# Bringing the score maxima of a two-stage attention kernel to rows through DRAM, beside the queries, with new first loads, fillings and ranks

## Chip, cores, metric

One core of a Trainium2 chip. The metric is the device time of the whole program in microseconds, the median of the runs shown. Engines are named as in the profile: PE (TensorE matmuls), PEld (its weight loads), DVE (VectorE), ACT (ScalarE), POOL (GpSimd), SP (SyncE, which here only issues DMAs).

## What is computed

16 sequences of 256 tokens, width 256, each with a context of 77 rows, all in float32. A first block applies to each sequence self-attention (16 heads of 16), cross-attention to its context and a gated MLP of width 1024, each with an RMS norm and a residual. A second block lets each normalised token attend to the normalised context (one head of 256), puts the result through a 4-wide GELU bottleneck, normalises, attends to itself and adds up.

```python
def attention(x, ctx, wq, wk, wv, wo):
    q = (x @ wq).reshape(B, S, NH, HD)
    k = (ctx @ wk).reshape(B, Skv, NH, HD)
    v = (ctx @ wv).reshape(B, Skv, NH, HD)
    scores = jnp.einsum('bqhd,bkhd->bhqk', q, k) * HD ** (-0.5)
    attn = jax.nn.softmax(scores.astype(jnp.float32), axis=-1)
    out = jnp.einsum('bhqk,bkhd->bqhd', attn, v).reshape(B, S, NH * HD)
    return out @ wo
...
h = residual + attention(h, h, sa_wq, sa_wk, sa_wv, sa_wo)
h = residual + attention(hn, context, ca_wq, ca_wk, ca_wv, ca_wo)
h = residual + mlp(hn, w_gate, w_up, w_down)
```

## The kernel before

**Stages.** Sequences (`b`, 0 to 15) go in pairs (`u`, UB = 2). The work of a sequence is cut into generators: `self_operands` (norm, transposition, q, k, v: tiles psq, psk, psv), `self_maxima`, `exponentials`, `outputs`, `projection` (wo), the same for the cross-attention (`cross_keys`, `cross_queries`, `cross_maxima`, tiles with a leading c), `mlp` (pg, pu, wd) and, per pair, `second_context` and `second`, which stores the result (L1192).

**The order** of all engines' instructions is written at build time by `Order.run` (L340). Each generator yields a `Step`: its PE time, its shape (f: full 128x128 array; r: four 32-row tiles; c: four 32-column tiles), the PSUM banks, the times of the other engines' instructions, what it needs and gives, and a lag. `Order` keeps a clock for each engine and takes the PE step that can start without being late, lowest rank first; the rank is the sequence number plus the stage's entry in `RANKS` (three numbers: always, for sequences 0 and 1, for the last three), plus `STANDS_BACK` for some changes of shape. `T_TURN` (L230) is the planned cost of a change of shape. Steps of other engines are put in between when they end within 500 ns of the best PE step's end (L360). SP's queue is in that order too: an issue that waits holds up all behind it. Where PE would wait, `keep_busy` (L326) issues matmuls on the identity (fillings, tile idle, L335).

**Softmax maxima.** Scores are computed twice. First with queries as rows (sc, L574, and csc, L600, row tiling: 32 rows for two heads), so that DVE can take each query's maximum, negated (L579, L607). The maxima of one sequence stand in a tile nmax, [128, 2, 128], query p of half i in partition p, with zeros between the 16 heads' columns. `maxima_rows` (L546) transposes both halves on PE (L551) into a bank, and two DVE instructions (L553) multiply that by the head masks and add it into qx, the masked queries, into rows which are zero there. kx holds ones in those rows, so the second score matmul (st and cst, L635; keys as rows) gives score minus maximum, and ACT's exponential (L643) writes pT, which `outputs` (L677) uses as it is. The four score banks (tile sc) are shared by all these and by parts of `second`.

**Transposed activations.** For sequences 0 and 1 `feature_major` transposes the normalised tokens on PE (L218). For all others DVE transposes 32x32 blocks (L429), SP writes them to DRAM (L434) and reads them back with the blocks in place (L439); the result is hnT. In the self-attention's hnT the two 128-feature chunks alternate element by element, in the others they stand 32 by 32. `project_T` reads hnT as the moving operand, `tokens_moving` in token order; psv reads it as weights (L748).

**First loads.** SP issues the four x tiles of sequences 0 and 1 with the first contexts between (L102 to L105). ACT's queue issues wq, wk, wv and wo (L152 to L155), POOL's sa_nw (L145), SP the rest. `weights` multiplies the norms' weights into the matrices (L1209). ACT's first own work is the square in `rmsnorm` (L377); the rstd in it is a power on POOL (L210), which also fills tiles by memset (L186 to L192).

Of the kernel before, what the change touches and what calls it, by code (L numbers as in the profile page):

```python
# [15 lines left out]
P = 128  # L16
D = 256
# [12 lines left out]
def kernel(  # L30
# [71 lines left out]
    for t in range(NT):  # L102
        if t == QT:
            cxs[0] = load_context(0, UB, "cx")
        load_tokens(0, t)  # L105

# [35 lines left out]

    ident = const.tile([P, P], F32, tag="ident", name="ident")
    make_identity(nc, ident)
    sa_nw = load_columns(sa_norm_w, "sa_nw", nc.gpsimd, True)  # L145
# [6 lines left out]
    wq = load_matrix(sa_wq, "wq", nc.scalar, True)  # L152
    wk = load_matrix(sa_wk, "wk", nc.scalar, True)
    wv = load_matrix(sa_wv, "wv", nc.scalar, True)
    wo = load_matrix(sa_wo, "wo", nc.scalar)  # L155
# [29 lines left out]
    for i in range(2):  # L185
        t = const.tile([SK, NH, 2 * HD], F32, tag=f"cvone{i}", name=f"cvone{i}")  # L186
        nc.gpsimd.memset(t, 1.0)
        cvones.append(t)
    for i in range(4):
        t = const.tile([P, QT, P], F32, tag=f"nmax{i}", name=f"nmax{i}")  # L190
        nc.gpsimd.memset(t, 0.0)
        maxes[i % 2].append(t)  # L192
# [42 lines left out]
    STANDS_BACK = {"rf": 5, "cf": 5, "fc": 10}  # L235
# [17 lines left out]
    class Order:  # L253
# [72 lines left out]
        def keep_busy(self, t):  # L326

            bank, after = self.banks["mm"][:2]
            n = int((t - self.clock["P"] - 350) / T_IDLE) if self.clock["P"] else FIRST_IDLE
            if n < 2 or None in bank + after or max(bank + after) > self.clock["P"]:  # L330
                return
            rows, cols = slice(RG if self.shape == "r" else P), slice(RG if self.shape == "c" else P)
            ps = mm_bank("idle")
            for _ in range(n):
                nc.tensor.matmul(  # L335
                    ps[cols, :P], lhsT=ident[rows, cols], rhs=ident[rows], start=True, stop=True
                )
            self.banks["mm"] = self.banks["mm"][1:] + [[t]]

        def run(self):  # L340
            while self.streams:
                best = None
                aux = []
                for st in self.streams:
                    t = self.start(st)
                    if t is None:
                        continue
                    if st.step.pe:
                        turn, wait = self.shape + st.step.shape, t - self.clock["P"]
                        late = wait > 100  # L350
                        rank = st.rank[0] + STANDS_BACK.get(turn, 0) + 0.05 * wait
                        key = (late, t + T_TURN[turn] if late else 0, rank, st.rank[1])
                        if best is None or key < best[0]:
                            best = (key, st, t)
                    else:
                        e = st.step.ops[0][0]
                        aux.append((max(t + T_NEXT, self.clock[e]), st.rank, st, t))
# [36 lines left out]
    def tokens_moving(t, c):  # L394

        return t[:, :, :, c].rearrange("p a i t -> p i a t")

# [148 lines left out]
    def maxima_rows(a, nm):  # L546

        yield Step(QT * T_TR, ops=[("V", 690), ("V", 690)], gives=[a.key("mT")])
        tp = mm_bank(f"{a.name}tm{a.b}")
        for i in range(QT):  # L550
            nc.tensor.transpose(tp[:, i * P : (i + 1) * P], nm[:, i, :], ident)  # L551
        for e in range(2):
            nc.vector.scalar_tensor_tensor(  # L553
                a.qx[:, :, e], bc_mid(tp[:, :S], NC), head_mask[:, 1 - e : 2 - e],
                a.qx[:, :, e], ALU.mult, ALU.add,
            )

    def maxima_of(nm, qt):

        return nm[:, qt].rearrange("p (j n d) -> p j n d", j=4, n=2 * NC)[:, :, :, 0]  # L560

    def self_maxima(a):
        for qt in range(QT):
            for c in range(NC):
# [4 lines left out]
                nm = maxes[0][a.b % 2]  # L569
                sc = sc_banks(f"sc{a.b}_{qt}{c}")  # L570
                for e in range(2):
                    for j in range(4):
                        rg = slice(RG * j, RG * (j + 1))
                        nc.tensor.matmul(  # L574
                            sc[:, j, (1 - e) * S : (2 - e) * S],
                            lhsT=a.qx[rg, c, e, qt * P : (qt + 1) * P],
                            rhs=a.kx[rg, c, e], start=True, stop=True,
                        )
# [9 lines left out]
    def cross_maxima(a):  # L588
        for qt in range(QT):
# [5 lines left out]
            nm = maxes[1][a.b % 2]  # L595
            sc = sc_banks(f"csc{a.b}_{qt}")
            for c in range(NC):
                for j in range(4):
# [5 lines left out]
                        lhsT=a.q[rg, c, qt * P : (qt + 1) * P],  # L604
# [84 lines left out]
    def projection(a):  # L689
# [21 lines left out]
        for i in range(QT):  # L711
# [11 lines left out]
    def self_operands(a):  # L723
# [3 lines left out]
        ps = yield from project_T(wq, lambda c: tokens_moving(hnT, c), S, f"psq{b}", in_halves(  # L727
# [64 lines left out]
    def cross_queries(a):  # L792
# [3 lines left out]
        ps = yield from project_T(cwq, lambda c: tokens_moving(hnT, c), S, f"pscq{b}", in_halves(  # L796
# [212 lines left out]
    def second(n, u, first, nb):  # L1009
# [164 lines left out]
        for kc in range(QT):  # L1174
            for t in range(NT):
# [37 lines left out]
    def context_loads():  # L1213
        for u in range(NU):
            yield Step(
                ops=[("S", 100)], acq=[("cx", u)], gives=[("cx", u)], lag=4000 if u else 6000
# [4 lines left out]
    def second_loads():  # L1221
        for u in range(NU):
            yield Step(ops=[("S", 100)], acq=[("cx2", u)], gives=[("cx2", u)], lag=4000)
            cx2s[u] = load_context(UB * u, UB, "cx2")
# [3 lines left out]
        ("x", 0): 5e3, ("x", 1): 20e3, "wq in": 8e3, "wk in": 9e3, "wv in": 10e3, "cwk": 12e3,  # L1228
# [19 lines left out]
        "mlp": (4.25, 2.75, -2.5),  # L1248
        "second_context": (5.5, 0, -50),
        "second": (3, 0, -50),  # L1250
# [71 lines left out]
```

## Time and profile before

| what | value |
|---|---|
| median of 3 runs | 995.84 us (995.49 to 997.2) |
| the profiled execution | 996.82 us, span 995.0 |
| mean granted clock of PE | 0.989 |
| busy PE / PEld / DVE / ACT / POOL | 97 / 72 / 63 / 48 / 9 % of the span |
| L551, maxima transposed on PE | 64 matmuls, 7.2 + 6.4 us busy |
| L553, maxima added into qx | 64 on DVE, 0.71 to 0.75 us each |
| L335, fillings | 198 matmuls, 32.5 us busy |
| DMA | 39.61 MB, mean 40 GB/s |

The span runs from the first to the last instruction. PE's matmuls are pipelined and their ends are modelled, so the time that one block of matmuls takes is better read as the distance from its start to the start of the next block than as its busy time. Instructions of float32 matmuls come in twos: eight make a projection of 256 x 256 for 256 tokens. Starts are in us from the span's beginning.

### The profile page before, as it was taken

To read this page: it belongs to the slowest core of one execution; us is meant where nothing else is said; L and a number is where in the kernel's file an instruction comes from. 1 tells how busy PE (TensorE), PEld (TensorE's weight loads), DVE (VectorE), ACT (ScalarE), POOL (GpSimd) and SP (SyncE) were. 2 spreads that over 40 slices of the span, in tenths; PEclk is the share of its full clock that TensorE was granted. 3 is DMA by queue.
4 is the path that set the end of the run, shared out by engine and by line. 5 is a ranking of instruction groups with operands and counts; after the bars stand their busy time and mean duration, and the time that the engine had idled before them with its cause. 6 is when DMAs were issued, how large, how long until landed. Compare 5 with 4: busy or idle time off the path is not lost.

```text
span 995.0 us, 18977 instructions
## 1 busy us (share of the span) xinstructions
PE 968.8 (97%) x8136; PEld 715.0 (72%) x8136; DVE 622.7 (63%) x1075; ACT 475.7 (48%) x770; POOL 93.7 (9%) x124
## 2 busy tenths in 40 slices
PE   7989999999999999999999999999999999999997
PEld 6766666676776667777776777777677777778876
DVE  4865576666675657766676655775578565655552
ACT  4246645334555364543755354454571526543432
POOL 2510000000010010100100000010020000100210
PEclk9899999999999999999999999999999999999997
DMA  8301001001000111002100121011210110001000
GB/s 275 82 24 39 22 11 40 2 22 32 29 23 22 42 61 43 12 33 77 43 12 22 46 83 46 1 33 35 64 54 1 49 33 23 32 12 54 12 22 22
DMA packets 45732, 39.61 MB, mean 40 GB/s; under 512 B 4336, under 2 KB 39760, under 8 KB 45648
## 3 DMA queue, kind: packets, MB, share of 16 engines
q1 hardware_dynamic: 44448, 37.34, 11.8%
q8 instruction: 64, 1.05, 0.4%
q10 hardware_dynamic: 1136, 1.05, 0.3%
q14 instruction: 20, 0.16, 0.1%
q0 software_dynamic: 64, 0.00, 0.0%
HBM read 23.14 MB, written 15.20 MB: 39 GB/s over the span
## 4 chain that ended last, share of the span: by engine, by line
PE 86%; DMA 4%; DVE 4%; ACT 4%; issue 1%; ACTq 0%; POOL 0%; SPq 0%; POOLq 0%
PE pg L828 11%; PE pu L828 11%; PE wd L858 11%; PE sc L574 6%; PE st L635 6%; PE po L677 5%; PE cst L635 3%; PE psq L499 3%; PE pscq L499 3%; PE wo L716 3%; PE cpo L677 3%; PE cwo L716 3%; PE psk L499 3%; PE psv L748 2%; PE csc L600 2%; ACT pT L643 2%
## 5 line engine op out<-in xcount | busy, mean ns | idle before, releaser
L579 DVE TENSOR_REDUCE nmax<-sc 128x8 f32<-128x2048 f32 x64 | 146.6, 2290 | 39.3 <-PE sc L574 39.2
L643 ACT ACTIVATE pT<-st 128x2048 f32<-128x2048 f32 x64 | 120.1, 1877 | 100.9 <-PE st L635 100.7
L828 PE MATMUL pg<-hnT_mlp,wg 128*128 128x256 f32 x512 | 129.8, 387 | 0.0
L828 PE MATMUL pu<-hnT_mlp,wu 128*128 128x256 f32 x512 | 128.7, 387 | 0.5 <-DVE sg L839 0.5
L858 PE MATMUL wd<-wd,gT 128*128 128x256 f32 x512 | 126.3, 388 | 0.0
L828 PEld LDWEIGHTS pu<-hnT_mlp,wu 128*128 128x128 f32 x512 | 93.4, 190 | 22.9 <-issue 10.6
L858 PEld LDWEIGHTS wd<-wd,gT 128*128 128x128 f32 x512 | 92.6, 190 | 23.8 <-issue 11.9
L828 PEld LDWEIGHTS pg<-hnT_mlp,wg 128*128 128x128 f32 x512 | 92.6, 190 | 21.0 <-issue 9.5
L643 ACT ACTIVATE cpT<-cst 77x2048 f32<-77x2048 f32 x32 | 59.9, 1872 | 59.2 <-PE cst L635 59.2
L838 ACT ACTIVATE sg<-pg 128x512 f32<-128x512 f32 x64 | 38.2, 597 | 101.5 <-PE pg L828 101.3
L839 DVE SCALAR_TENSOR_TENSOR sg<-sg,pg 128x512 f32<-128x512 f32 x64 | 43.9, 686 | 67.2 <-ACT sg L838 66.7
L677 PE MATMUL po<-pT,vone 128*32 128x256 f32 x1024 | 62.7, 382 | 0.1
L840 DVE SCALAR_TENSOR_TENSOR gT<-sg,pu 128x512 f32<-128x512 f32 x64 | 43.7, 683 | 28.5 <-PE pu L828 27.4
L607 DVE TENSOR_REDUCE nmax<-csc 128x16 f32<-128x1232 f32 x32 | 46.1, 1440 | 8.3 <-PE csc L600 8.0
L677 PEld LDWEIGHTS po<-pT,vone 128*32 128x32 f32 x1024 | 29.7, 109 | 26.0 <-issue 9.7
L210 POOL TENSOR_TENSOR rstd_n<-ve_n,neg_half 128x4 f32<-128x4 f32 (+3 forms) x28 | 23.4, 837 | 206.2 <-DVE ve_n L208 160.6
L210 POOL TENSOR_TENSOR rstd_ca<-ve_ca,neg_half 128x2 f32<-128x2 f32 x16 | 11.1, 697 | 304.7 <-DVE ve_ca L208 304.6
L335 PE MATMUL idle<-ident 128*128 128x128 f32 (+2 forms) x198 | 32.5, 327 | 2.5 <-POOL ident masks.py:199 2.5
L499 PE MATMUL pscq<-hnT_ca,cwq 128*128 128x256 f32 x128 | 31.7, 388 | 2.4 <-DMA hnT_ca<-blocks_ca 2.4
L499 PE MATMUL psk<-hnT_sa,wk 128*128 128x256 f32 x128 | 33.4, 397 | 0.0
L499 PE MATMUL psq<-hnT_sa,wq 128*128 128x256 f32 x128 | 33.4, 399 | 0.0
L335 PEld LDWEIGHTS idle<-ident 128*128 128x128 f32 (+2 forms) x198 | 30.7, 228 | 3.5 <-POOL ident masks.py:199 2.5
(614 smaller groups left out, 1570.8 us busy)
## 6 DMA issues: line engine op xcount, KB each, us to landing
h<-in_x_dram SPq DMA_DIRECT2D x7, 512.0 KB
blocks_sa<-hb_sa SPq DMA_DIRECT2D x14, 256.0 KB
hnT_sa<-blocks_sa SPq DMA_DIRECT2D x14, 256.0 KB
blocks_ca<-hb_ca SPq DMA_DIRECT2D x14, 256.0 KB
hnT_ca<-blocks_ca SPq DMA_DIRECT2D x14, 256.0 KB
blocks_mlp<-hb_mlp SPq DMA_DIRECT2D x14, 256.0 KB
hnT_mlp<-blocks_mlp SPq DMA_DIRECT2D x14, 256.0 KB
out_dram<-h SPq DMA_DIRECT2D x7, 512.0 KB
```

What stands on the lines that cost most here:

```text
L335: nc.tensor.matmul(ps[cols, :P], lhsT=ident[rows, cols], rhs=ident[rows], start=True, stop=True)
L499: nc.tensor.matmul(ps[:, m * n : (m + 1) * n], lhsT=w[:, c, m * P : (m + 1) * P], rhs=src(c), start=(c == 0), stop=(c == NC - 1),)
L574: nc.tensor.matmul(sc[:, j, (1 - e) * S : (2 - e) * S], lhsT=a.qx[rg, c, e, qt * P : (qt + 1) * P], rhs=a.kx[rg, c, e], start=True, stop=True,
L579: nc.vector.tensor_reduce(maxima_of(nm, qt)[:, :, c::NC], sc.rearrange("p j (y k) -> p j y k", y=2), AX.X, ALU.max, negate=True,)
L607: nc.vector.tensor_reduce(maxima_of(nm, qt), sc[:, :, : 2 * NC * SK].rearrange("p j (n k) -> p j n k", k=SK), AX.X, ALU.max, negate=True,)
L635: nc.tensor.matmul(st[:nk, j, e * S : (e + 1) * S], lhsT=a.kx[rg, c, e, kc * P : kc * P + nk], rhs=a.qx[rg, c, e], start=True, stop=True,)
L643: nc.scalar.activation(a.pT[k][:nk].rearrange("p j e q -> p j (e q)"), st[:nk], AF.Exp, scale=HD ** -0.5,)
L677: nc.tensor.matmul(po[RG * j : RG * (j + 1), e, :], lhsT=a.v[:nk, kc, 8 * c + 2 * j + e, :], rhs=pT[:nk, j, e, :], start=(kc == 0 and e == ...
L716: nc.tensor.matmul(ps[:, i * D : (i + 1) * D], lhsT=oT[:, c, i * P : (i + 1) * P], rhs=a.w[:, c, :], start=(c == 0), stop=(c == NC - 1),)
L828: nc.tensor.matmul(ps[:, i * S : (i + 1) * S], lhsT=w[:, c, (f + i) * P : (f + i + 1) * P], rhs=tokens_moving(hnT, c), start=(c == 0), sto ...
L839: nc.vector.scalar_tensor_tensor(sg, sg, 1.0, ps, ALU.add, ALU.mult)
L858: nc.tensor.matmul(ps[:, :D], lhsT=gT[:, f, i * P : (i + 1) * P], rhs=wd[:, f, :], start=(f == 0), stop=(f == NF - 1),)
```

## The change

The maxima of sequences 2 to 15 no longer go through PE. Their nmax is [128, 2, 32] with 16 used columns; DVE transposes it in 32x32 blocks, SP writes it to DRAM, and four SP reads put the rows straight into the zero rows of qx. Query position 2p+i now holds token 128i+p (`tokens_paired`, and steps of two, `qt::QT`, in the weight loads that must give token order back). Sequences 0 and 1 keep the transposition on PE, with their four wide nmax in one tile.

```diff
     def maxima_rows(a, nm):
-        yield Step(QT * T_TR, ops=[("V", 690), ("V", 690)], gives=[a.key("mT")])
-        tp = mm_bank(f"{a.name}tm{a.b}")
-        for i in range(QT):
-            nc.tensor.transpose(tp[:, i * P : (i + 1) * P], nm[:, i, :], ident)
...
+        if a.b < UB:
+            yield Step(QT * T_TR, ops=[("V", 690), ("V", 690)], gives=[a.key("mT")])
+            tp = mm_bank(f"{a.name}tm{a.b}")
+            for i in range(QT):
+                nc.tensor.transpose(tp[:, i:S:QT], nm[:, i, :], ident)
...
+            return
+        name = f"{a.name}nm{a.b}"
+        yield Step(ops=[("V", 140)])
+        nb = small.tile([P, RG, QT], F32, tag="nmb", name=f"{name}b")
+        nc.vector.transpose(nb.rearrange("p t i -> p i t"), nm)
+        yield Step(ops=[("S", 500)], gives=[name], lag=2000)
+        rows = dram.tile([P, RG * QT], F32, tag="rows", name=f"{name}r")
+        nc.sync.dma_start(rows, nb.rearrange("p t i -> p (t i)"))
+        yield Step(ops=[("S", 2000)], needs=[name], gives=[a.key("mT")], lag=2000)
+        by_row = rows.rearrange("(g w) x -> w g x", w=RG)
+        for n in range(2 * NC):
+            y, c = divmod(n, NC)
+            nc.sync.dma_start(
+                a.qx[RG // 4 * n :: RG, c, 1 - y].rearrange("j (g x) -> j g x", x=RG * QT),
+                by_row[n : 8 * NC : 2 * NC],
+            )
...
+    def tokens_paired(t, c):
+        return t[:, :, :, c].rearrange("p a i t -> p a t i")
...
-                            lhsT=a.qx[rg, c, e, qt * P : (qt + 1) * P],
+                            lhsT=a.qx[rg, c, e, qt::QT],
...
-                        lhsT=a.q[rg, c, qt * P : (qt + 1) * P],
+                        lhsT=a.q[rg, c, qt::QT],
...
-                    ps[:, i * D : (i + 1) * D], lhsT=oT[:, c, i * P : (i + 1) * P],
+                    ps[:, i * D : (i + 1) * D], lhsT=oT[:, c, i::QT],
...
-        ps = yield from project_T(wq, lambda c: tokens_moving(hnT, c), S, f"psq{b}", in_halves(
+        ps = yield from project_T(wq, lambda c: tokens_paired(hnT, c), S, f"psq{b}", in_halves(
...
-        ps = yield from project_T(cwq, lambda c: tokens_moving(hnT, c), S, f"pscq{b}", in_halves(
+        ps = yield from project_T(cwq, lambda c: tokens_paired(hnT, c), S, f"pscq{b}", in_halves(
```

The first loads are in another order: SP takes the two x tiles of sequence 0, then sa_nw, wk, wv, the x tiles of sequence 1, the contexts and wo; ACT's queue keeps only wq.

```diff
+    for t in range(QT):
+        load_tokens(0, t)
...
+    wq = load_matrix(sa_wq, "wq", nc.scalar, True)
+    sa_nw = load_columns(sa_norm_w, "sa_nw", nc.sync, True)
+    wk = load_matrix(sa_wk, "wk", nc.sync, True)
+    wv = load_matrix(sa_wv, "wv", nc.sync, True)
+    for t in range(QT, NT):
+        load_tokens(0, t)
+    cxs[0] = load_context(0, UB, "cx")
+    wo = load_matrix(sa_wo, "wo", nc.sync)
...
+    wide = pool.tile([P, 4, QT, P], F32, tag="lp", name="nmax", bufs=1)
+    nc.gpsimd.memset(wide, 0.0)
```

In the planner: fewer fillings in long gaps and some in shorter ones; no T_TURN in the choice among late steps; SP's steps stand aside while PE's clock is behind them; 800 for 500; the out store is a step of its own; other due times of the first loads; other ranks.

```diff
-    STANDS_BACK = {"rf": 5, "cf": 5, "fc": 10}
+    STANDS_BACK = {"rf": 5, "cf": 5, "fc": 5}
...
-            n = int((t - self.clock["P"] - 350) / T_IDLE) if self.clock["P"] else FIRST_IDLE
-            if n < 2 or None in bank + after or max(bank + after) > self.clock["P"]:
+            n = int((0.7 * (t - self.clock["P"]) - 150) / T_IDLE) if self.clock["P"] else FIRST_IDLE
+            if n < 1 or None in bank + after or max(bank + after) > self.clock["P"]:
...
-                        key = (late, t + T_TURN[turn] if late else 0, rank, st.rank[1])
+                        key = (late, t if late else 0, rank, st.rank[1])
...
+                        b = max(t + T_NEXT, self.clock[e])
+                        (ahead if e == "S" and b > self.clock["P"] else aux).append(
+                            (b, st.rank, st, t)
+                        )
+                if not best and not aux:
+                    aux = ahead
...
-                    if best is None or b + sum(o[1] for o in st.step.ops) <= best[2] + best[1].step.pe + 500:
+                    if best is None or b + sum(o[1] for o in st.step.ops) <= best[2] + best[1].step.pe + 800:
...
-        yield Step(460, "r", "sc", ops=[("V", 70 + 290 * NT)], rel=[("h", u)] * (first + nb == UB),
-                   gives=[("second", n)])
+        yield Step(460, "r", "sc", ops=[("V", 70 + 290 * NT)], gives=[("second", n)])
         nc.vector.tensor_tensor(h, h, by_rows(zT, k["last"], "out"), ALU.add)
+        yield Step(ops=[("S", 600)], rel=[("h", u)] * (first + nb == UB), lag=3000)
         nc.sync.dma_start(tokens(out, u)[:, first * QT : first * QT + NT], h)
...
-        "second_constants": (1, 50, 0),
-        "outputs": (6.5, -1, 50),
+        "second_constants": (-49, 0, 0),
+        "outputs": (6.5, -51, 50),
...
-        "projection": (-0.5, -50, -0.5),
-        "cross_outputs": (5, 0, 0.25),
+        "projection": (-0.5, -50, 1.5),
+        "cross_outputs": (5, 2, 0.25),
...
-        "cross_projection": (-50.5, 0, 50),
-        "self_maxima": (-0.25, -50, -100),
-        "cross_maxima": (-49, 0, 0),
-        "cross_queries": (-2, 1, -49.5),
-        "self_operands": (-2, 0, -0.5),
-        "cross_keys": (1.75, 0, 0),
-        "mlp": (4.25, 2.75, -2.5),
-        "second_context": (5.5, 0, -50),
-        "second": (3, 0, -50),
+        "cross_projection": (-51.5, 0, 50),
+        "self_maxima": (-0.25, -50, -101),
+        "cross_maxima": (-99, 0, 0),
+        "cross_queries": (1, -49, -49.5),
+        "self_operands": (-2, 0, 0.5),
+        "cross_keys": (0.75, 0, 2),
+        "mlp": (4, 0.75, 0.5),
+        "second_context": (5.5, 0, 0),
+        "second": (5, 0, -50),
```

More of the change, by code (lines that the diff above doesn't have):

```diff
@@ L100, in load_context @@
         return t
[L102 to L105, printed above, removed]
     def tokens_of(b):
@@ L141, in row @@
         return src.rearrange("(o d) -> o d", o=1)
+    for t in range(QT):
+        load_tokens(0, t)
     ident = const.tile([P, P], F32, tag="ident", name="ident")
     make_identity(nc, ident)
-    sa_nw = load_columns(sa_norm_w, "sa_nw", nc.gpsimd, True)
+    wq = load_matrix(sa_wq, "wq", nc.scalar, True)
[6 more added lines that the diff above has]
+    wo = load_matrix(sa_wo, "wo", nc.sync)
     vones, cvones, maxes = [], [], ([], [])
@@ L151 @@
         vones.append(t)
[L152 to L155, printed above, removed]
     load_tokens(1)
@@ L188 @@
         cvones.append(t)
+    rows_of = ([], [])
+    wide = pool.tile([P, 4, QT, P], F32, tag="lp", name="nmax", bufs=1)
+    nc.gpsimd.memset(wide, 0.0)
     for i in range(4):
-        t = const.tile([P, QT, P], F32, tag=f"nmax{i}", name=f"nmax{i}")
+        maxes[i % 2].append(wide[:, i])
+        t = const.tile([P, QT, RG], F32, tag=f"nmax{i}", name=f"nmax{i}")
         nc.gpsimd.memset(t, 0.0)
-        maxes[i % 2].append(t)
+        rows_of[i % 2].append(t)
     def bc_mid(t, n):
@@ L342, in run @@
                 best = None
-                aux = []
+                aux, ahead = [], []
                 for st in self.streams:
@@ L356, in run @@
                         e = st.step.ops[0][0]
-                        aux.append((max(t + T_NEXT, self.clock[e]), st.rank, st, t))
+                        b = max(t + T_NEXT, self.clock[e])
[4 more added lines that the diff above has]
+                    aux = ahead
                 if aux:
                     b, _, st, t = min(aux, key=lambda a: a[:2])
-                    if best is None or b + sum(o[1] for o in st.step.ops) <= best[2] + best[1].step.pe + 500:
+                    if best is None or b + sum(o[1] for o in st.step.ops) <= best[2] + best[1].step.pe + 800:
                         self.put(st, t)
@@ L546, in maxima_rows, with maxima_tile @@
     def maxima_rows(a, nm):
-        yield Step(QT * T_TR, ops=[("V", 690), ("V", 690)], gives=[a.key("mT")])
-        tp = mm_bank(f"{a.name}tm{a.b}")
-        for i in range(QT):
[L551 to L555, printed above, removed]
-            )
+        if a.b < UB:
[3 more added lines that the diff above has]
+                nc.tensor.transpose(tp[:, i:S:QT], nm[:, i, :], ident)
+            for e in range(2):
+                nc.vector.scalar_tensor_tensor(
+                    a.qx[:, :, e], bc_mid(tp[:, :S], NC), head_mask[:, 1 - e : 2 - e],
+                    a.qx[:, :, e], ALU.mult, ALU.add,
+                )
[14 more added lines that the diff above has]
+                by_row[n : 8 * NC : 2 * NC],
+            )
+    def maxima_tile(a):
+        return (maxes if a.b < UB else rows_of)[bool(a.name)][a.b % 2]
     def maxima_of(nm, qt):
-        return nm[:, qt].rearrange("p (j n d) -> p j n d", j=4, n=2 * NC)[:, :, :, 0]
+        wide = nm.shape[-1] == P
+        return nm[:, qt, : P if wide else 16].rearrange(
+            "p (j n d) -> p j n d", j=4, n=2 * NC
+        )[:, :, :, 0]
     def self_maxima(a):
@@ L568, in self_maxima @@
                 )
-                nm = maxes[0][a.b % 2]
+                nm = maxima_tile(a)
                 sc = sc_banks(f"sc{a.b}_{qt}{c}")
@@ L594, in cross_maxima @@
             )
-            nm = maxes[1][a.b % 2]
+            nm = maxima_tile(a)
             sc = sc_banks(f"csc{a.b}_{qt}")
@@ L1215, in context_loads @@
             yield Step(
-                ops=[("S", 100)], acq=[("cx", u)], gives=[("cx", u)], lag=4000 if u else 6000
+                ops=[("S", 100)], acq=[("cx", u)], gives=[("cx", u)], lag=(10000, 20000)[u] if u < 2 else 4000
             )
@@ L1222, in second_loads @@
         for u in range(NU):
-            yield Step(ops=[("S", 100)], acq=[("cx2", u)], gives=[("cx2", u)], lag=4000)
+            yield Step(ops=[("S", 100)], acq=[("cx2", u)], gives=[("cx2", u)], lag=4000 if u > 1 else 20000)
             cx2s[u] = load_context(UB * u, UB, "cx2")
@@ L1227 @@
     order.done.update({
-        ("x", 0): 5e3, ("x", 1): 20e3, "wq in": 8e3, "wk in": 9e3, "wv in": 10e3, "cwk": 12e3,
+        ("x", 0): 4e3, ("x", 1): 20e3, "wq in": 5e3, "wk in": 6e3, "wv in": 7e3, "cwk": 12e3,
         "cwv": 13e3, "cwq in": 16e3, "wg in": 24e3, "wu in": 27e3, "wd": 24e3, "late": 14e3,
```

## Prediction

> **What bounds the kernel now.** I read the page's busy times first, then the busy times by stretch, then TensorE's own timeline, then the start and the end. The profiled execution took 996.82 us with a span of 995.0, so 1.82 us lie outside the span; the median of the runs shown is 995.84. I work out differences in the span and take them off the median.
>
> ```profile
> PE 968.8 (97%) x8136; PEld 715.0 (72%) x8136; DVE 622.7 (63%) x1075; ACT 475.7 (48%) x770; POOL 93.7 (9%) x124
> ...
> DMA  8301001001000111002100121011210110001000
> ```
>
> Only PE is full. VectorE has a third of the span free and the DMA engines are nearly idle after the first two slices: a change that moves work from PE to those two pays if nobody waits for the detour.
>
> ```profile
> 0.00:25.00 25.00, 19.81 (x116) 17.09 (x116) 11.18 (x28) 11.69 (x29) 5.69 (x18) 1.00 0.90 274
> ...
> 300.00:400.00 100.00, 99.87 (x854) 71.77 (x852) 63.78 (x109) 51.43 (x83) 6.22 (x9) 1.00 0.13 42
> ...
> 950.00:995.00 45.00, 36.77 (x212) 28.63 (x210) 17.81 (x61) 10.81 (x20) 3.76 (x5) 0.84 0.07 24
> ```
>
> The columns are stretch, length, busy PE, PEld, DVE, ACT, POOL, granted clock, DMA share, GB/s. In the middle PE never stops, so only removed PE time counts there. The ends are chains: PE idles, or runs the fillings of L335, which the first column counts as busy.
>
> **Part 1: maxima of sequences 2 to 15 leave PE.** 14 sequences x 2 attentions = 28 blocks of two transposes (L551) go. What one is worth is read from starts, since PE durations overlap:
>
> ```profile
> 154.29 1.03 PE L828 MATMUL pu<-hnT_mlp,wu 128*128 128x256 f32 x4
> 155.15 0.38 PE L551 MATMUL tm<-ident,nmax 128*128 128x128 f32 x2
> 155.46 1.15 PE L574 MATMUL sc<-kx__973,qx__907 32*128 32x256 f32 x16
> ```
>
> The block holds PE from 155.15 to 155.46, 0.31 us. But four pu matmuls before a full-array successor take 0.86 (154.29 to 155.15) and before a row-tiled one 0.95 (171.40 to 172.35): 0.09 of the 0.31 is the turn to row tiling, which the block before will then pay. So 0.22 each, and 28 x 0.22 = **6.1 us** saved. Blocks that follow a row-tiled step hold 0.27 and leave their turn to their successor in the same way.
>
> On VectorE 28 x 2 x 0.745 (the STTs of L553) = 41.7 us go. 28 small transposes come: 128x128 takes 0.31 and 128x512 0.70 (L1151, L429), so a line through both gives 0.25 for 64 columns, 7 us in all. VectorE is no bound; I count nothing, between 0 and -2.
>
> New on SP: one write and four reads per block, 140 DMAs. An issue takes 0.33 (L434) to 0.73 (L923), so 46 to 102 us of a queue that issued some 120 DMAs and mostly waits. The reads wait for the write to land; behind them on SP stand loads of hnT, for which PE waits. A 256 KB write lands 2.0 us after its issue when nothing disturbs it (the chain shows 3.5), its read after 2.7 (chain: 2.9 to 3.9). Path from the last maximum to usable rows: 0.25 + 0.35 + 2.0 + 4 x 0.33 + 2.7 = 6.6 us, where the transposes and STTs needed some 2 to 3. I read for each of the 28 the end of its last maximum and the start of its first score matmul (L635): 12 have over 6.6 us already, 16 have 2.3 to 5.9. Those 16 lack 39 us together. The order gives each step a due time, and mlp, projection and output matmuls of other sequences stand ready, so I take 0 with bounds 0 and +39. Without that cover it is rival B.
>
> The out store becomes a step of its own and SP steps are put off while PE is behind them, so that SP is less often parked in front of a load. PE waits that ended with a load of hnT_ca sum to 2.4 us and psq's weight load waited 0.4. I take **-1.2**, bounds -2.8 and 0; the loss side is B's.
>
> **Part 2: queries in pairs.** So that one row of a DRAM block is 64 neighbouring positions, position 2p+i holds token 128i+p. Three readers change.
> (a) The weight loads of sc, csc and wo step by 8 bytes. psv does that today: 195 ns against 189 for pscq, and its matmuls keep their pace. In wo it is hidden; in 64 sc and 32 csc visits at most one 6 ns load is in front: **+0.6**, bounds 0 and +2.3 (four loads in front).
> (b) The moving operand of psq and pscq (128 instructions each) now jumps 256 bytes back and forth. No row shows PE reading so. Nearest: psq already steps by 8 bytes and pscq does not; from 183.20 to 185.11 psq needs 1.91 per eight, pscq 1.80 (169.60 to 171.40), both after a row-tiled step and before a full one. By start-to-start that is 10 to 14 ns per instruction for half the neighbours. I price the next halving alike: +10 on psq, +20 on pscq, 128 x 0.010 + 128 x 0.020 = **+3.8 us**. Lower end 0 (a moving read can't gain from jumps). Upper end: ACT's L387 for sequences 0 and 1 reads and writes in 16-byte steps and takes up to 0.758 where the plain one takes 0.50: 0.25 per 256 elements, 256 x 0.25 = +64. I keep near the PE row, since it is the same engine and the same line.
>
> A rule speaks against (b). The Trainium skill, "SBUF — State Buffer", section "Door 1: The DMA port swizzle", says that SBUF has lines of 16 bytes, that at least two consecutive hits on a line are needed for full rate, and that each access to another line pays. The paired read has one hit per line; psq's 8-byte step has two and should be free by the rule, where the row shows 10 ns. The page gives no price; at half rate for PE it would make the sum rival A's 1037, by the PE row 986.
>
> **Part 3: the start.** ACT's queue issues wq, wk, wv and wo, and only then its first work:
>
> ```profile
> 0.75 1.28 ACTq L116 DMA_DIRECT2D wq<-in_L_xattn_sa_wq_dram  x2
> ...
> 6.98 0.41 ACTq L120 DMA_DIRECT2D wo<-in_L_xattn_sa_wo_dram  x1
> 7.42 1.28 ACT L377 ACT_TABLE_LOAD   x1 [7.42 <-DMA wv<-in_L_xattn_sa_wv_dram]
> ...
> 8.71 0.42 ACT L377 ACTIVATE sq_sa<-h 128x256 f32<-128x256 f32 x1
> ...
> 13.26 2.05 PE L499 MATMUL psq<-hnT_sa,wq 128*128 128x256 f32 x8
> ```
>
> With wq alone on it, ACT is free at 2.03, the table is loaded by 3.3 and the square can start there: the first x tile, issued at 0.74, landed at 2.8. From square to psq takes 4.55, so psq at about 8; rstd on POOL then queues behind the memsets (to 5.0 now; one wide one and four small more, but sa_nw's 1.3 of issuing gone) and may lose half a microsecond: 8.5 instead of 13.26, 4.7 earlier. sa_nw, now on SP, is due at 5 to 5.5 and does not bind. The price is the second pair of x tiles, cx and wo behind wk and wv. What follows (scores, maxima, exponentials up to 130) is a dependent chain and should shift along; I count **-4.0**, bounds -4.7 and 0 (DMA is 90% busy to 25, so something later may arrive no earlier).
>
> **Part 4: fillings.** Their number falls from (gap-350)/220 to (0.7 gap-150)/220. Two hold up work now:
>
> ```profile
> 975.50 6.15 PE L335 MATMUL idle<-ident 128*128 128x128 f32 x32
> ...
> 978.84 0.25 DVE L1113 COPY mga<-mg 128x12 f32<-128x12 f32 x2
> 981.48 0.27 PE L1124 MATMUL tp_g2T<-ident,g 128*64 128x128 f32 x1
> ```
>
> The operands are there at 979.1, PE comes free at 981.4. 16 fillings mean a gap of about 3.9 us by the plan, so the new count is 11: five fewer of 0.37 each, **-1.9**. Near 34.5 ten fillings end at 38.3 while VectorE freed the bank at 37.2: seven instead, **-1.0**. The clock there is already reduced (0.84 in the last stretch, 0.86 from 25 to 50); fewer fillings may reduce it elsewhere. Bounds together: -3.3 and +2.
>
> **Part 5: ranks, STANDS_BACK, the term T_TURN, 800 for 500.** They re-order; nothing is added or removed. In the middle they can change only the number of turns at about 0.1 us per side, and nearly every row-tiled step already stands alone, because the four score banks are emptied in 1.9 to 2.3 us before the next. At the ends they can fill or open gaps. The constants of the second stage move up (rank 51 to -49); their small issues on SP, 0.22 to 1.28 each and now at 23 to 34, can then stand before the first loads of hnT_sa. I take 0, bounds -12 (all 19 us of fillings before 130 can't go, the tail has some 10) and +6.
>
> **Sum**: -6.1 -1.2 +0.6 +3.8 -4.0 -2.9 = -9.8. The span becomes 985.2, the profiled execution 987.0, and the median **986.0**.
>
> **Rivals.**
> *A, paired reads are dear.* At half rate each 216 ns instruction costs 216 more: 256 x 0.216 = 55 in place of 3.8, so 1037. It decides from 53 ns per instruction ((9.8 + 3.8)/256). For it: ACT's L387. Against: PE's step from 4 to 8 bytes cost 10 ns only, and PE takes a 4-byte element every 0.84 ns (216/256), no fast rate. 8%.
> *B, rows come late* (the slower side I think most of). The scores wait on SP's chain of write, landing, four reads, or hnT loads stand behind it. All 39 us uncovered gives 1025, a half 1005; it ends slower from 12 us, 0.7 for each of the 16. For it: L439 has waited for its write 37 times already. Against: PE is full from 150 to 950 with lists of ready work. 10%.
> *C, the new order also fills the ends.* Of the 19 us of fillings before 130 and the chain after 965, some 12 go: 974. For it: ranks of sequences 0 and 1 and of the last three are what changed most. Against: those chains are of dependent steps. 22%.
> *D, given back.* The early start is lost to DMA, the transposes' time goes into turns: 995. 6%.
> The forecast itself, 978 to 993.8: 54%.
>
> Under 0.2%, or 2.0 us, can't be told from no change here. Faster: 54 + 22 = 76%; within 0.2%: 6%; slower: 18%. The range for 8 in 10 goes from 969 (C with its bounds) to 1001, the mild half of B; A and the rest of B stay out.
>
> **What would show it.** Right: only 8 maxima transposes, all for sequences 0 and 1; psq first near 8.5; the sum of PE's idle time after 150 not over 15 us; psq and pscq within 1.85 to 2.05 per eight; first filling of the last chain shorter by five. Wrong: psq over 2.4 per eight (A); score matmuls or pscq waiting for DMA by over 10 us in sum (B); fillings before 130 under 8 us (C).

## The result and the profile after

The changed kernel takes 1006.99 us (median of 6 runs, 1005.44 to 1009.67) against 996.52 for the kernel before on the same chip (6 runs): **a ratio of 1.0106, 95% interval 1.009 to 1.0121, so slower**, where 986.0 was forecast. Its profiled execution took 1005.78 us with a span of 1004.0. Of the after page, the busy times and the DMA line of the slices:

```profile
PE 977.4 (97%) x8044; PEld 708.3 (71%) x8044; DVE 592.4 (59%) x1047; ACT 473.2 (47%) x770; POOL 92.7 (9%) x123
...
DMA  8300100001100111002110031001210020020000
```

PE issues 92 matmul instructions fewer (56 transposes and 36 fillings) and is busy 8.6 us longer. VectorE lost 30.3 us of work and the DMA engines are as idle as before. So dearer matmuls, not a new queue, are the first thing to look for. The page's costliest groups name them (instruction, shape, count, busy us, mean ns, idle before):

```profile
L515 PE MATMUL psq<-hnT_sa,wq 128*128 128x256 f32 x128 | 46.6, 512 | 4.5 <-DVE last L957 4.4
...
L515 PE MATMUL pscq<-hnT_ca,cwq 128*128 128x256 f32 x128 | 38.5, 442 | 0.0
L515 PE MATMUL psk<-hnT_sa,wk 128*128 128x256 f32 x128 | 33.6, 394 | 0.0
```

The three have the same shape and the same line of code. psk still reads tokens in order and takes 394 ns (397 before); psq was at 399 and pscq at 388. Ends are modelled, so the price is better read from starts. PE's timeline of the kernel before:

```profile
169.60 1.97 PE L499 MATMUL pscq<-hnT_ca,cwq 128*128 128x256 f32 x8 [1.17 <-DMA hnT_ca<-blocks_ca]
171.40 1.03 PE L828 MATMUL pu<-hnT_mlp,wu 128*128 128x256 f32 x4
...
183.20 2.08 PE L499 MATMUL psq<-hnT_sa,wq 128*128 128x256 f32 x8
185.11 0.38 PE L551 MATMUL ctm<-ident,nmax 128*128 128x128 f32 x2
```

and of the kernel after:

```profile
182.94 2.43 PE L515 MATMUL pscq<-hnT_ca,cwq 128*128 128x256 f32 x8
185.20 1.03 PE L898 MATMUL wd<-wd,gT 128*128 128x256 f32 x4
...
187.24 2.87 PE L515 MATMUL psq<-hnT_sa,wq 128*128 128x256 f32 x8
189.95 1.07 PE L515 MATMUL psk<-hnT_sa,wk 128*128 128x256 f32 x4
```

Eight pscq now hold PE for 2.26 us and eight psq for 2.71, for 1.80 and 1.91 before. From start to start of single instructions inside the blocks psq went from 226 to 327 ns and pscq from 216 to 270: **128 x 0.101 + 128 x 0.054 = 19.8 us**.

Busy times by stretch, in the columns of the forecast's first table:

```profile
0.00:25.00 25.00, 22.99 (x128) 17.89 (x132) 14.20 (x31) 13.29 (x32) 6.22 (x19) 1.00 0.82 263
...
100.00:130.00 30.00, 27.91 (x234) 19.65 (x227) 17.91 (x23) 13.18 (x28) 2.10 (x3) 0.77 0.10 33
300.00:400.00 100.00, 100.00 (x861) 71.32 (x860) 59.58 (x113) 54.80 (x90) 9.96 (x12) 1.00 0.15 48
...
```

The middle is full, as before: from 300 to 400 PE never stops, so it waits for no rows there. What is new is PE's clock (the third number from the right) between 100 and 130: 0.77, where the kernel before ran at full clock:

```profile
100.00:130.00 30.00, 27.94 (x298) 19.88 (x297) 13.92 (x20) 20.51 (x29) 2.07 (x3) 1.00 0.06 19
```

The first column counts a slowed matmul as busy just the same; only the clock column shows it.

The start, from the after kernel's timeline of all engines:

```profile
2.03 1.28 ACT L389 ACT_TABLE_LOAD   x1 [2.03 <-issue]
...
3.32 0.42 ACT L389 ACTIVATE sq_sa<-h 128x256 f32<-128x256 f32 x1
...
8.75 2.87 PE L515 MATMUL psq<-hnT_sa,wq 128*128 128x256 f32 x8
...
36.45 0.39 SPq L455 DMA_DIRECT2D hnT_sa<-blocks_sa  x1
...
39.40 3.75 PE L515 MATMUL psq<-hnT_sa,wq 128*128 128x256 f32 x8 [4.43 <-DVE last L957]
```

The first psq starts 4.5 us earlier (8.75 for 13.26). The psq of sequence 2 starts at 39.40 for 41.05: 1.65 earlier. Between the two PE now stands still for 4.43 us. The profile puts that wait down to VectorE's L957, whose tile psq does not read; the read of hnT_sa issued at 36.45, which psq does need, is the likelier cause, and in the second timing of experiment 2's kernel the same wait is put down to it.

### The profile page after: what moved, and what is told of

Read it like the earlier page. It is cut to its first block, busy times and chain, and to the rows that moved or that the text cites. A ratio compares the mean times of both kernels' runs of the same rounds, so it can differ in the third digit from the quotient of the medians.

```text
span 1004.0 us, 19053 instructions
## 1 busy us (share of the span) xinstructions
PE 977.4 (97%) x8044; PEld 708.3 (71%) x8044; DVE 592.4 (59%) x1047; ACT 473.2 (47%) x770; POOL 92.7 (9%) x123
## 3 DMA queue, kind: packets, MB, share of 16 engines
q1 hardware_dynamic: 51856, 39.51, 12.6%
## 4 chain that ended last, share of the span: by engine, by line
PE 88%; DVE 5%; ACT 3%; DMA 2%; SPq 1%; issue 1%; POOL 0%; POOLq 0%; ACTq 0%; DVEq 0%
PE pg L868 12%; PE pu L868 11%; PE wd L898 11%; PE st L675 7%; PE sc L614 6%; PE po L717 6%; PE psq L515 4%; PE pscq L515 3%; PE cst L675 3%; PE cpo L717 3%; PE wo L756 3%; PE cwo L756 3%; PE psk L515 2%; PE psv L788 2%; PE csc L640 2%; DVE nmax L619 2%
## 5 line engine op out<-in xcount | busy, mean ns | idle before, releaser
L868 PEld LDWEIGHTS pu<-hnT_mlp,wu 128*128 128x128 f32 x512 | 94.3, 190 | 22.6 <-issue 10.3
L898 PEld LDWEIGHTS wd<-wd,gT 128*128 128x128 f32 x512 | 92.2, 190 | 21.8 <-issue 10.9
L515 PE MATMUL psq<-hnT_sa,wq 128*128 128x256 f32 x128 | 46.6, 512 | 4.5 <-DVE last L957 4.4
L515 PEld LDWEIGHTS psq<-hnT_sa,wq 128*128 128x128 f32 x128 | 24.5, 202 | 20.2 <-DVE last L957 4.7
L515 PE MATMUL pscq<-hnT_ca,cwq 128*128 128x256 f32 x128 | 38.5, 442 | 0.0
L903 DVE TENSOR_TENSOR h<-h,wd 128x256 f32<-128x256 f32 x32 | 13.3, 416 | 38.1 <-PE wd L898 38.1
```

The source lines that it names most:

```text
L515: nc.tensor.matmul(ps[:, m * n : (m + 1) * n], lhsT=w[:, c, m * P : (m + 1) * P], rhs=src(c), start=(c == 0), stop=(c == NC - 1),)
L868: nc.tensor.matmul(ps[:, i * S : (i + 1) * S], lhsT=w[:, c, (f + i) * P : (f + i + 1) * P], rhs=tokens_moving(hnT, c), start=(c == 0), sto ...
L898: nc.tensor.matmul(ps[:, :D], lhsT=gT[:, f, i * P : (i + 1) * P], rhs=wd[:, f, :], start=(f == 0), stop=(f == NF - 1),)
```

## Experiments

The question was first whether the paired reads alone explain the loss (theory T1), or the late rows, the new order or the start do (rivals). Ratios are to the kernel before, run on the same chip, with 95% intervals.

**1. Only the pairs, in the old kernel** (x1_before_pairs). Order, loads, maxima on PE: all as before.

```diff
-        ps = yield from project_T(wq, lambda c: tokens_moving(hnT, c), S, f"psq{b}", in_halves(
+        ps = yield from project_T(wq, lambda c: tokens_paired(hnT, c), S, f"psq{b}", in_halves(
...
-                            lhsT=a.qx[rg, c, e, qt * P : (qt + 1) * P],
+                            lhsT=a.qx[rg, c, e, qt::QT],
```

(and likewise pscq, csc, wo and the columns of tm.)

> The kernel before with the queries in pairs and nothing else: paired moving reads for psq and pscq, weight loads in steps of two for sc, csc and wo, maxima still transposed on PE, order of the instructions unchanged. Theory 1 (the paired reads are dear, and by themselves more than the whole loss): psq 327 ns start to start, pscq 270, as in the changed kernel, so 128 x 0.101 + 128 x 0.054 + 0.8 = +20.6 us in a full PE: 1017. Theory 2 (the new order and late rows lose the time; the reads only fill what would be waiting): under +5, 1001 at most.

Measured: 1014.71 us, ratio 1.0185 (1.0169 to 1.0201), **+19.05 us**. The same groups on its page:

```profile
L503 PE MATMUL psq<-hnT_sa,wq 128*128 128x256 f32 x128 | 46.1, 505 | 0.3 <-DMA hnT_sa<-blocks_sa 0.3
...
L503 PE MATMUL pscq<-hnT_ca,cwq 128*128 128x256 f32 x128 | 38.7, 443 | 1.7 <-DMA hnT_ca<-blocks_ca 1.7
```

The slowdown of both groups is there with nothing else changed, and the time from start to start that they gained (psq +12.6 us, pscq +6.8) is the whole loss. T1 holds.

**2. The whole change, but pairs that lie in order in memory** (x2_after_contig). hnT of the self-attention and of the cross-attention is written by DVE and the DMAs with the two token halves next to each other, so that the paired order is one step through memory; q, k and v of the self-attention then all use it. Nothing else moves.

```diff
-        return t[:, :, :, c].rearrange("p a i t -> p (a i t)")
+        return t[:, :, :, c].rearrange("p a i t -> p (a t i)")
...
-        by_tokens = kind == "sa"
+        dims = {"sa": "t i c", "ca": "c t i", "mlp": "i c t"}[kind]
...
-        shape = [P, P // RG, QT] + ([RG, NC] if by_tokens else [NC, RG])
+        shape = [P, P // RG] + [size[d] for d in dims.split()]
```

> The changed kernel with hnT stored so that the paired order is read with one step: two halves next to each other in the cross-attention's hnT (step 4 bytes), and all of q, k and v in paired order in the self-attention's (step 8 bytes, as psq had before). VectorE's block transposes write in other steps; DMA sizes are unchanged. Theory 1: psq back to 226 ns, pscq to 216, 1007 - 19.8 = 987, which is 1% under the kernel before. Theory 2: PE waits instead, 1003 to 1007.

Measured: 988.96 us, 0.9923 (0.9907 to 0.994). The same kernel was timed once more, beside other runs of the kernel before:

> The changed kernel with hnT stored in pairs once more, in five rounds beside the kernel before, for its interval: 0.9925 of the time before if the reads were all that was wrong with the change, 1.0 or more if the first look was chance.

Measured: 988.58 us, 0.9919 (0.9894 to 0.9943). From 10.5 us above the kernel before to 6.7 below it: taking the jumps away is worth 17.2 us and makes the change a gain. VectorE pays for it with 5.3 us of work off PE's path (597.7 us busy for 592.4). The page of this second timing has the old durations back:

```profile
L519 PE MATMUL psq<-hnT_sa,wq 128*128 128x256 f32 x128 | 34.5, 412 | 2.5 <-DMA hnT_sa<-blocks_sa 2.3 <-ACT hnT_sa L441 0.3
...
L519 PE MATMUL pscq<-hnT_ca,cwq 128*128 128x256 f32 x128 | 31.6, 389 | 0.0
```

**3. What about the read is dear** (x3_micro_reads). A kernel that holds nothing of the attention: 12 matmuls (24 instructions) for each order of reading 256 elements.

```diff
+        ("by16", 1024, lambda: b[:, 0:1024:4]),
...
+        ("next16", 256, lambda: b[:, 0:256].rearrange("p (u i v) -> p u v i", i=2, v=4)),
...
+        ("asca", 512, lambda: b[:, 0:512].rearrange("p (a i c t) -> p c a t i", a=4, i=2, c=2)[:, 0]),
...
+        ("far512", 256, lambda: b[:, 0:256].rearrange("p (i t) -> p t i", i=2)),
...
```

> No attention at all: twelve matmuls each with one 128x128 weight tile and 256 moving columns in thirteen read orders; x is copied to the output. Start to start of one instruction. Line theory (each read from another 16-byte line than the one before costs): steps of 4 and 8 bytes 216 and 226, steps of 16 and 32 at least the 270 of pscq, inline (0,2,1,3 in one line) 216, next16 and next32 (back and forth between two lines) 270 or more, asca 270, assa 327, run2 between, run4 216. Jump theory (only jumps back, or far jumps, cost): by16 and by32 under 240, inline and next16 dear like asca.

PE's timeline of it (names without their numbers, so "by" holds by8, by16 and by32, "next" and "run" two each):

```profile
22.15 5.34 PE L44 MATMUL one<-big,wt 128*128 128x256 f32 x24
27.33 27.46 PE L44 MATMUL by<-big,wt 128*128 128x256 f32 x72
54.61 5.36 PE L44 MATMUL inline<-big,wt 128*128 128x256 f32 x24
59.81 13.17 PE L44 MATMUL next<-big,wt 128*128 128x256 f32 x48
72.82 6.72 PE L44 MATMUL asca<-big,wt 128*128 128x256 f32 x24
79.37 8.04 PE L44 MATMUL assa<-big,wt 128*128 128x256 f32 x24
87.25 6.73 PE L44 MATMUL far<-big,wt 128*128 128x256 f32 x24
93.81 10.78 PE L44 MATMUL run<-big,wt 128*128 128x256 f32 x48
104.43 5.34 PE L44 MATMUL again<-big,wt 128*128 128x256 f32 x24
```

A block's time is the distance to the next start: asca (the order of pscq after the change) (79.37 - 72.82)/24 = 273 ns, assa (that of psq) (87.25 - 79.37)/24 = 328, one 216. The single starts split the rest:

| order of reading | ns per instruction | 16-byte lines touched |
|---|---|---|
| in order (one, again) | 216 | 64 |
| steps of 8 / 16 / 32 bytes | 227 / 451 / 460 | 128 / 256 / 256 |
| 0, 2, 1, 3 inside one line (inline) | 216 | 64 |
| back and forth, 16 / 32 / 512 bytes | 273 / 269 / 273 | 64 |
| pscq's order (asca) | 273 | 64 |
| psq's order (assa): back and forth, with 8-byte steps | 328 | 128 |
| runs of 8 / 16 bytes back and forth, 512 bytes apart | 227 / 216 | 64 |

Half of the line theory stands: a new line for each element (by16) doubles the time, and a changed order inside one line (inline) is free. The other half falls: going back and forth changes the line just as often and is much cheaper, and the width of the jump does not matter. The jump theory falls as a whole, since by16 never jumps back and is the dear one. In the kernel, psq was at 226 and went to 327, pscq from 216 to 270: the bench gives 227 to 328 and 216 to 273. So the cause of the 19 to 20 us is shown in three ways: alone in the old kernel, by its removal from the new one, and apart from both.

The remaining runs ask about the rest of the change, which gives -6.7 us (experiment 2) where the forecast's other terms sum to -13.6.

**4. Part 1 without the new order** (x4_before_dram): the kernel before, with the maxima through DRAM and experiment 2's storage, old ranks, loads, fillings and planner.

```diff
+        name = f"{a.name}nm{a.b}"
+        yield Step(ops=[("V", 140)])
+        nb = small.tile([P, RG, QT], F32, tag="nmb", name=f"{name}b")
+        nc.vector.transpose(nb.rearrange("p t i -> p i t"), nm)
+        yield Step(ops=[("S", 500)], gives=[name], lag=2000)
...
```

> The kernel before with part 1 of the change alone: maxima of sequences 2 to 15 through DRAM, queries in pairs, but hnT stored so that the pairs are read with one step; old first loads, old planner, old ranks and old fillings. Theory 1: -6.1 for the transposes, +0.8 for the weight loads, and nothing lost to late rows: 991. Theory 2 (rows come late): at or over the time before, with score matmuls or hnT loads that wait for DMA by more than 5 us in sum.

Measured: 1027.25 us, 1.0318 (1.0298 to 1.0339). Missed by 36 us, and on the slower side. PE's timeline there shows how the time goes:

```profile
...
909.33 3.44 PE L340 MATMUL idle<-ident 128*32 128x128 f32 x30
912.70 1.99 PE L512 MATMUL pscq<-hnT_ca,cwq 128*128 128x256 f32 x8
914.53 1.89 PE L753 MATMUL cwo<-cwo,coT__7650 128*128 128x256 f32 x8
916.35 0.82 PE L637 MATMUL csc<-cckm__7040,ccqT__7680 32*128 32x154 f32 x16
916.99 1.72 PE L340 MATMUL idle<-ident 32*128 32x128 f32 x14
```

Fillings appear far from both ends: the planner had no ready work. 332 filling instructions in place of 198 hold PE, from start to start, for 58.1 us in place of 35.3. The sign of theory 2 is there too: PE's waits that end with a load of hnT or of rows sum to 6.7 us (5.2 of them pg's for hnT_mlp). SP's queue in the same stretch has the steps of Part 1 (a write, then four reads) between the writes and reads of hnT, one chain behind the other:

```profile
907.51 0.33 SPq L447 DMA_DIRECT2D blocks_ca<-hb_ca  x1
909.57 0.37 SPq L452 DMA_DIRECT2D hnT_ca<-blocks_ca  x1
921.37 0.33 SPq L579 DMA_DIRECT2D cnm15r<-cnm15b  x1
922.90 2.21 SPq L584 DMA_DIRECT2D ccqx__7682<-cnm15r  x4
925.15 0.44 SPq L447 DMA_DIRECT2D blocks_mlp<-hb_mlp  x1
927.28 0.38 SPq L452 DMA_DIRECT2D hnT_mlp<-blocks_mlp  x1
```

**5. Everything but the ranks** (x8_contig_oldranks): experiment 2 with `RANKS` and `STANDS_BACK` of before, to see whether it is the ranks that hide the detour.

```diff
-    STANDS_BACK = {"rf": 5, "cf": 5, "fc": 5}
+    STANDS_BACK = {"rf": 5, "cf": 5, "fc": 10}
...
-        "cross_maxima": (-99, 0, 0),
-        "cross_queries": (1, -49, -49.5),
+        "cross_maxima": (-49, 0, 0),
+        "cross_queries": (-2, 1, -49.5),
...
-        "second": (5, 0, -50),
+        "second": (3, 0, -50),
```

> As the changed kernel with hnT stored in pairs (989.0), but with the old ranks and STANDS_BACK; the new rules for SP steps, the new loads and fillings stay. Part 1 alone in the old order took 1027 with 12 us of fillings from 909 to 930. Theory A (rows through DRAM come late and only the new ranks leave work to cover that): 1010 to 1025. Theory B (the new rules for SP's steps and the store as its own step do it): 987 to 995.

Measured: 1012.89 us, 1.0177 (1.0152 to 1.0202), 24 us above experiment 2. The slices of its fillings (busy tenths) have work missing in the middle again, and those of experiment 2's kernel (the second) have not:

```profile
busy tenths in 40 slices 3111400000000000000000000001100200000007
```

```profile
busy tenths in 40 slices 4211400000000000000000000000000000000007
```

So with the new ranks (and `STANDS_BACK`) the detour costs nothing that shows, and without them the kernel takes 24 us more. Between 150 and 950 us the old ranks bring 8.2 us of fillings for 0.8 and 6.2 us more of other pauses of PE. That it is late rows which the new ranks cover is not shown: no wait of PE in this run is put down to rows, and where fillings stand before a score matmul that reads rows (cst at 800.74), the four reads of these were issued from 791.12 to 793.34, 7 us earlier.

**6. Everything but Part 1** (x9_contig_pe): experiment 2 with all maxima back on PE.

```diff
-        if a.b < UB:
+        if True:
...
-        return (maxes if a.b < UB else rows_of)[bool(a.name)][a.b % 2]
+        return maxes[bool(a.name)][a.b % 2]
```

(The four wide nmax also get a place of their own again.)

> As the changed kernel with hnT stored in pairs (989.0), but the maxima of all sequences go through PE and VectorE as before the change: 28 blocks of two transposes come back, no DMA for maxima; new loads, planner, ranks and fillings stay. Theory of the prediction's part 1 (28 x 0.22 = 6.1 us of PE, rows covered under the new ranks): 995. Rival (without the DRAM path no step waits long for its maxima, and these ranks order at least as well): 989 or less.

Measured: 1008.3 us, 1.0117 (1.0092 to 1.0141): 19.7 above experiment 2, more than either side expected. The transposition blocks alone take 9.1 us back (12.3 for 3.1, by starts). The sc blocks take 3.0 and the cwo blocks 2.7 us more, and one place shows how, with VectorE in front of PE:

```profile
110.13 1.15 PE L615 MATMUL sc<-kx__668,qx__639 32*128 32x256 f32 x16
114.23 1.41 PE L641 MATMUL csc<-cckm__295,ccqT__1081 32*128 32x154 f32 x16 [2.95 <-DVE nmax L620]
115.57 3.78 PE L757 MATMUL cwo<-cwo,coT__1104 128*128 128x256 f32 x8
...
110.49 1.40 DVE L571 SCALAR_TENSOR_TENSOR qx__430<-tm,head_mask,qx__430 128x512 f32<-128x512 f32 x2
111.81 2.28 DVE L620 TENSOR_REDUCE nmax<-sc 128x8 f32<-128x2048 f32 x1
```

PE waits 2.95 us for banks that VectorE empties by its reduction at 111.81, after two instructions (1.40 us) that the PE path needs and the DRAM path does not; the granted clock is 0.50 from 115.57 to 119.28, and the eight cwo there take 3.71 us in place of 1.84. The ranks fit the DRAM path and not the old one; ranks tuned again for the PE path were not tried.

**7. The small parts**, each undone in experiment 2's kernel: the constants' rank (x5_contig_oldsecond), the formula for fillings (x6_contig_oldfill), the first loads with their due times (x7_contig_oldloads).

```diff
-        "second_constants": (-49, 0, 0),
+        "second_constants": (1, 50, 0),
```

> As the changed kernel with hnT stored in pairs (989.0), but with the rank of the constants of the second stage as before (51 for -49). In that kernel PE waits 4.75 us at 28.5 for a load of these constants and 2.75 us at 38 for VectorE behind them. Theory: these waits are what the early start is lost to; without them the start's gain stays, 983 to 985. Rival: the first 40 us are bound by DMA, something else waits as long, 988 to 990.

```diff
-            n = int((0.7 * (t - self.clock["P"]) - 150) / T_IDLE) if self.clock["P"] else FIRST_IDLE
-            if n < 1 or None in bank + after or max(bank + after) > self.clock["P"]:
+            n = int((t - self.clock["P"] - 350) / T_IDLE) if self.clock["P"] else FIRST_IDLE
+            if n < 2 or None in bank + after or max(bank + after) > self.clock["P"]:
```

> As the changed kernel with hnT stored in pairs (989.0), but with the old number of fillings, (gap-350)/220 and at least two. Theory of the prediction: the fillings hold up work, so +2.9: 992. Rival: the shorter fillings let the granted clock fall to half more often (33, 40, 78, 108 and 125 us in that kernel, only 35 in the one before), so the old number gains: 985 to 987.

```diff
-    wk = load_matrix(sa_wk, "wk", nc.sync, True)
-    wv = load_matrix(sa_wv, "wv", nc.sync, True)
...
+    wk = load_matrix(sa_wk, "wk", nc.scalar, True)
+    wv = load_matrix(sa_wv, "wv", nc.scalar, True)
+    wo = load_matrix(sa_wo, "wo", nc.scalar)
...
-        ("x", 0): 4e3, ("x", 1): 20e3, "wq in": 5e3, "wk in": 6e3, "wv in": 7e3, "cwk": 12e3,
+        ("x", 0): 5e3, ("x", 1): 20e3, "wq in": 8e3, "wk in": 9e3, "wv in": 10e3, "cwk": 12e3,
```

> As the changed kernel with hnT stored in pairs (989.0), but with the first loads in the old order and with the old due times: psq first near 13.3 for 8.7. Theory of the prediction: the start is a chain, +4.0: 993. Rival: PE has waits to fill up to 130 us in any case, so the gain of the start is lost again, within 1.5 of 989.

Measured: 989.45 (0.995, 0.9931 to 0.9969), 991.5 (0.9945, 0.9926 to 0.9963) and 991.79 (0.9957, 0.994 to 0.9974). The twelve runs of experiment 2's kernel have a median of 988.85 us, so undoing these parts costs 0.6, 2.7 and 2.9 us. The first can't be told from nothing by its time: in x5 PE still waits 4.0 us for fc_sb, so the constants' rank is not what makes that late. For the fillings 991.5 lies near its theory's 992 and not at the rival's 985 to 987, but the interval overlaps both of experiment 2's. For the loads it barely meets them (0.994 to 0.9974 against 0.9907 to 0.994 and 0.9894 to 0.9943), so the new loads are likely worth some 2 to 3 us at the end: less than the theory's 4.0, more than the rival's 1.5. But the traces do not show this gain as a lead that is kept. PE's timeline of x7, with the old loads:

```profile
41.31 2.05 PE L518 MATMUL psq<-hnT_sa,wq 128*128 128x256 f32 x8 [0.41 <-DVE qx__231 L573]
59.31 2.08 PE L518 MATMUL psq<-hnT_sa,wq 128*128 128x256 f32 x8
```

and of x10, with the new ones:

```profile
32.73 0.37 PE L941 MATMUL tp_fc<-ident,fc_sb 4*128 4x4 f32 x2 [3.96 <-DMA fc_sb<-in_L_xattn_fc_w_dram]
...
40.52 3.58 PE L519 MATMUL psq<-hnT_sa,wq 128*128 128x256 f32 x8 [2.29 <-DMA hnT_sa<-blocks_sa]
...
59.62 2.08 PE L519 MATMUL psq<-hnT_sa,wq 128*128 128x256 f32 x8
```

The first psq starts at 13.6 in x7 and at 9.0 in x10. At sequence 2 the lead of 4.6 us is down to 0.8, at sequence 3 it is gone (59.31 and 59.62): with the new loads PE waits 3.96 + 2.29 us in between, and the eight psq after that pause take 3.51 from start to start, where eight take 1.91 at full clock; the granted clock there is 0.53 (40.5 to 44).

## Why the prediction was wrong

**The step that failed is 2(b)**, the moving operand of psq and pscq: "I price the next halving alike: +10 on psq, +20 on pscq, 128 x 0.010 + 128 x 0.020 = +3.8 us". Measured: +101 and +54 ns, 19.8 us in the trace, 19.05 alone in the old kernel, 17.2 when taken out of the new one. The row that the price rested on, a step of 8 bytes, still takes two elements of each 16-byte line one after the other; the paired read takes one and leaves. These are different cases (227 against 273 and 328 ns in experiment 3), and the one does not extrapolate to the other. With 16 us more in this term the same sum gives 1002 in place of 986.0, beyond the range's 1001; 1006.99 was measured. The row at the upper end was misread as well: L387 writes in 16-byte steps but reads in order, so it is no row of such a read. The error in rank is telling too: the forecast has pscq dearer than psq, but psq reads twice as many lines.

Rival A had the right mechanism and the wrong size: 77 ns per instruction on average, beyond its deciding point of 53 and far below its price of 216. Between a cheap near row and a dear far one there was a wide gap, and the deciding point lay in it; 8% was too little for that gap. The forecast's own sign for A, psq over 2.4 us per eight, is what came (2.71).

**Part 1** was right in its own terms: the tm blocks fell from 10.5 to 2.9 us by starts, -7.6 for -6.1, with the turns partly paid by neighbours, and pscq's 2.4 us of waits for hnT_ca are gone. "So I take 0" for the 16 late rows holds in this kernel, but not for the reason given. The forecast trusted that the order always has ready work; experiments 4 and 5 show that with the old ranks it has not: x8 takes 24 us more than experiment 2's kernel, x4 32 more than the kernel before. Rival B is seen in x4, in the 6.7 us of waits for loads; Part 5 is what keeps that loss away, and how much of it is late rows stays open. "They re-order; nothing is added or removed", with bounds of -12 and +6, was therefore wrong as a term of its own: Parts 1 and 5 have one price together, and apart each costs (x4, x9).

**Part 2(a)**: eight-byte weight steps made a score visit 8 ns longer (sc 1076 to 1084, csc 740 to 748), about 0.8 us in 64 + 32 visits, near the forecast (+0.6).

**Part 3**: psq at 8.75, forecast 8.5. But "What follows is a dependent chain and should shift along" fails: SP's queue still has to issue the second stage's constants first, and the DMA engines are 0.82 busy up to 25 us. VectorE had the blocks of sequence 2 ready at 29.5, SP issued their write at 33.32, behind the last constants, and the hnT_sa read at 36.45 for 37.53, only 1.1 us earlier. PE arrives early at loads that are not early, and experiment 7 shows the lead used up within 60 us. That is rival D's first half, in this term alone. By time, x7 still leaves some 2 to 3 of the 4.0 us at the end; how they get there the traces do not show.

**Part 4**: as counted, the last chain's first block of fillings is 24 instructions for 32 (12 fillings where 11 were worked out) and holds PE for 3.06 us in place of 5.98:

```profile
987.40 2.92 PE L341 MATMUL idle<-ident 128*128 128x128 f32 x24
990.46 0.30 PE L1164 MATMUL tp_g2T<-ident,g 128*64 128x128 f32 x1
```

In the median this can't be resolved (experiment 7). The warning beside that step, that fewer fillings may reduce the clock elsewhere, points to a likely part of the rest. Each run records its span and its mean clock; span times one minus the clock is the clock time lost. Its median is 10.9 us in 43 runs of the kernel before and 14.3 in the 12 runs of experiment 2's kernel, and in both the span grows by about 0.7 us for each microsecond lost (straight lines, correlation 0.8). At no loss the lines give 987.4 and 977.1: -10.3. So some 2.4 to 3.6 of the missing 7 us go with the clock, lost now between 100 and 150 us too, where PE is the bound (0.83 and 0.90 in the two halves of that stretch in the after kernel), while the kernel before ran there at 1.00. The same line through the ten runs of x7 gives 978.0 at no loss, with a median of 17.8 us lost: by it, most of what the new loads are worth comes by the clock, and 0.9 us otherwise. This is a fit and not an experiment; that pauses such as the 2.95 us in x9 bring the clock down is seen in single places only, and which part of the change makes them is open.

Without the term 2(b) the forecast's sum is -13.6 and the measurement -6.7. If the fit holds, the 3.1 us of the start's 4.0 that are not kept and the clock's 0.7 x 3.4 = 2.4 make up 5.5 of the 6.9 between them; no run shows that split, and the rest is open. **Undoing the one mis-sized step turns the change into the gain that was forecast in sign**: experiment 2's kernel beats both, by 0.8% and 1.8%.

## What to carry to other kernels

Before an access pattern of a full TensorE is changed, count how many elements it takes in a row from each 16 bytes; if it is one, measure that read by itself, since neighbours with two in a row tell nothing of it. Where a DMA already rearranges the operand, let it write the order in which PE will read: here that cost only 5.3 us of VectorE's free time and was worth 17 us. A detour that lengthens a chain and the order that goes with it had one price here; a forecast should price them together, and not trust a rank list that was tuned for one path on another.

## What the hardware showed

In experiment 3 the extra time over 216 ns follows the number of different lines that are left after a single element: 64 such lines cost 53 to 57 ns, 128 (assa) 112, 256 (by16) 235, some 0.9 ns for each line, however often it is come back to and whether the jump goes 16 or 512 bytes. Two elements in a row nearly remove it (by8 and the 8-byte runs, 11 ns), four do (0), and a changed order inside one line is free. That the chip keeps the lines that it has just left is only a way to read the table.

The Trainium skill, "SBUF — State Buffer", section "Door 1: The DMA port swizzle", asks for at least two hits on a 16-byte line for full rate. by16, with one hit (451 for 216), agrees, and the 8-byte runs, with two, come within 5% of full rate (227). Its conclusion that four float32 can be stepped over for free does not agree: a step of four elements doubles the time here.
